# Two stacked cross-attention layers: queries, keys and maxima split into high and low halves, scores and maxima from single-pass products

## The chip, the cores and the metric

The kernel runs on one core of a Trainium2 chip. The time is the device time of one execution in microseconds (us). Three runs of the kernel before gave 947.76 to 949.83 us, with a median of 949.11 us.

## The reference

```python
def layer(x, ctx, Wq, Wk, Wv, Wo, bo):          # x 32x256x320, ctx 32x77x512
    q = heads(x @ Wq)                            # 20 heads of 16 channels
    k, v = heads(ctx @ Wk), heads(ctx @ Wv)
    p = softmax(q @ k.T / sqrt(16), axis=-1)     # 256 x 77 for each head
    return merge_heads(p @ v) @ Wo + bo + x
x = layer(x, ctx, *L0)
x = layer(x, ctx, *L1)
```

All inputs and outputs are float32. The extra key and value weights of the two modules (object, others, ip) meet no rows here, since the context has 77 positions, and they add nothing.

## The kernel before, in words

**Units.** One unit is one layer for one pair of the 32 batch entries: 16 pairs by two layers are 32 units, numbered `u` in an order in which layer 1 of a pair follows its layer 0 by several units. A unit's 20 heads lie in five groups `g` of four head pairs. A head pair takes 32 partitions, so that one group fills the 128 partitions: row group `j` (32 partitions) holds the two heads `e` = 0 and 1 of one pair, 16 channels each.

**Steps of a unit.** `keys` and `keys_rest` project the context to keys (tile kR, by way of the PSUM banks psk). `queries`, or `outputs_and_queries` together with the output projection of the unit three places earlier, project x to queries (tile q0; banks psq and psy). `mask_keys` (L257) makes kT, keys with the other head's 16 rows zeroed, for the maxima. `less_keys` (L267) makes kM, which has the same zeros but a row of minus ones in one of the other head's rows. `maxima` (L455) multiplies 128 queries at a time (as weights) by kT into the banks psm, and VectorE reduces them to the largest score of each query. `turn` (L484) transposes those maxima and sends them by eight DMAs into one row of q0 and q1, each of which holds all the query channels; that row meets the minus ones of kM. So `scores` (L497) yields score minus maximum (banks pss) from one float32 product for each head, ScalarE takes exp into pT, `products` multiplies by the values (banks po), and `divide` and `turn_back` normalise and transpose into oT. q1 is a DMA copy of q0 (lines 339, 349, 385).

**Products.** Each float32 product appears in the profile as two pairs of a weight load (LDWEIGHTS, on the engine row PEld) and a matmul. Four products that use different row groups (or different 32-column strips) run beside each other; below, four such records make a *round*. A group's scores are eight products, or four rounds of 256 columns with 77-column weights. The maxima of one half of a group (`h`, ten to a unit, 128 queries each) are four products, or two rounds of 154 columns with 128-column weights. A unit has ten such halves.

**Order.** `tc.manual_schedule()` leaves the order to the program. It is written out in *slots*: `at(slot, where, step)` files a step, and within a slot steps run in this order:

```python
order = (
    "load", "maxima", "turn back", "turn", "scores", "values", "rest", "back", "full", "last",
)
```

`start(u)` is the slot of a unit's first scores; four units take 17 slots. Queries of unit u are made at the end ("full") of slot s = start(u-2), and its maxima follow from slot s+1 on, two or three halves to a slot, once the unit before has had its own. All engines run their instructions in this order, each waiting on semaphores. TensorE, ScalarE (ACT), VectorE (DVE) and GpSimd (POOL) have a queue each. SyncE (SP) issues nearly all DMAs, in order too, so that a DMA that waits for its data holds those behind it. PSUM has eight banks, taken in turn: four for psm, four for pss, one for po, and so on. Before unit 0's first scores in slot 0 there are ten slots, from -10 on, that fill the pipeline (the *prologue* below); each makes what a later one needs.

Of the kernel before, what the change touches and what calls it, by code (L numbers as in the profile page):

```python
# [52 lines left out]
F32 = mybir.dt.float32  # L53
AF = mybir.ActivationFunctionType
# [12 lines left out]
SCALE = 1.0 / HD**0.5  # L67

# [26 lines left out]
def xattn_kernel(ctx: ExitStack, tc: tile.TileContext, xT, cT, cP, weights, outT):  # L95
# [16 lines left out]
    def load_x(p):  # L112
        x_sb = io.tile([P, NX], F32, tag="x", name=f"x_{p}", bufs=AHEAD + 3)
        xs[p] = x_sb
        if p == 0:
            for a, b in ((0, NT), (NT, 2 * NT), (2 * NT, NX)):
                nc.sync.dma_start(out=x_sb[:, a:b], in_=xT[p, :, a:b])
        else:
            (nc.scalar if p == 1 else nc.sync).dma_start(out=x_sb, in_=xT[p])

    def load_context(u):
        p = units[u][0]
        c_sb = cs[u] = io.tile([P, NKA, NB * L], F32, tag="c", name=f"c_{u}", bufs=3)
# [33 lines left out]
    stages, maxes = [[], []], []  # L157
    for layer in range(2):
        for i in range(2):
# [3 lines left out]
            stages[layer].append(v)  # L163
    for i in range(2):
        m = const.tile([P, 2 * NG, 32], F32, name=f"max_{i}")
        nc.gpsimd.memset(m, 0.0)
        maxes.append(m)
# [6 lines left out]
    masks = const.tile([P, 2], F32, name="masks")  # L174
    nc.vector.tensor_reduce(masks, r32.rearrange("p (e d) -> p e d", d=HD), AX.X, ALU.add)

    less = const.tile([P, 2], F32, name="less")
    for e in range(2):
        i = HD * (1 - e)
        nc.vector.tensor_scalar_mul(less[:, e : e + 1], r32[:, i : i + 1], -1.0)  # L180
# [76 lines left out]
    def mask_keys(u, t):  # L257

        kR, groups = st[u]["kr"], slice(2 * t, min(2 * t + 2, NG))
        n = groups.stop - groups.start  # L260
        kT = work.tile([P, 2, n, L], F32, tag=f"kT{t}", name=f"kT_{u}_{t}", bufs=2)
        st[u]["k", t] = kT
        engine = nc.gpsimd if u else nc.vector
        for e in range(2):
            engine.tensor_scalar_mul(kT[:, e], kR[:, groups], masks[:, e : e + 1])  # L265

    def less_keys(u):  # L267

        kR = st[u].pop("kr")
        kM = st[u]["km"] = work.tile([P, 2, NG, L], F32, tag="kM", name=f"kM_{u}", bufs=3)  # L270
        for e in range(2):
            nc.gpsimd.tensor_scalar(
                kM[:, e], kR, masks[:, e : e + 1], less[:, e : e + 1], ALU.mult, ALU.add
            )

    def keys(u, t):
        p, layer = units[u]
        w, c_sb = w_sb[layer], cs[u]
        if t == 0:
            st[u]["kr"] = work.tile([P, NG, L], F32, tag="kR", name=f"kR_{u}", bufs=2)  # L280
        kR = st[u]["kr"]
# [9 lines left out]
        nc.scalar.copy(kR[:, 2 * t : 2 * t + 2].rearrange("p g k -> p (g k)"), ps[:, 0 : 2 * L])  # L291
        mask_keys(u, t)

    def keys_rest(u):
# [14 lines left out]
        nc.scalar.copy(st[u]["kr"][:, 4], ps[:, 0:L])  # L309
        mask_keys(u, 2)  # L310

    def new_queries(u):
        st[u]["q"] = [
            work.tile([P, NX], F32, tag=f"q{e}", name=f"q{e}_{u}", bufs=3) for e in range(2)
        ]
        return st[u]["q"][0]

    def queries(u):
# [19 lines left out]
        if u > 0:  # L338
            nc.sync.dma_start(out=st[u]["q"][1], in_=q0)

    def queries_rest(u):
# [3 lines left out]
        q0, q1 = st[u]["q"]  # L345
# [3 lines left out]
        nc.sync.dma_start(out=q1, in_=q0)  # L349

    def outputs_and_queries(u, uq):
# [33 lines left out]
        nc.sync.dma_start(out=st[uq]["q"][1], in_=q0)  # L385
# [44 lines left out]
    def place_vals(u, i):  # L430

        p, layer = units[u]
        if "v" not in st[u]:
            st[u]["v"] = work.tile(
                [P, NB, HEADS // 2, 2, 2, HD], F32, tag="v", name=f"v_{u}", bufs=3
# [19 lines left out]
    def maxima(*parts):  # L455
# [3 lines left out]
        for i, (u, h) in enumerate(steps):  # L459
            g, c = h // 2, h % 2  # L460
            q, kT = of_group(st[u]["q"][0], g), st[u]["k", g // 2]
            for j in range(4):
                r = slice(32 * j, 32 * j + 32)
                nc.tensor.matmul(  # L464
                    ps[j][:, i * 2 * L : (i + 1) * 2 * L],
                    q[r, c * P : (c + 1) * P],
# [365 lines left out]
```

## Time and profile before

| what | value |
|---|---|
| three runs, us | 947.76, 949.11, 949.83 |
| profiled execution: span from first to last instruction, us | 947.2 |
| time of that execution outside its span | not shown by the page; the median of the runs is 1.9 us over the span |
| TensorE matmuls (PE) busy | 940.9 us, 99% |
| TensorE weight loads (PEld) busy | 630.3 us, 67% |
| VectorE (DVE) busy | 533.2 us, 56% |
| ScalarE (ACT) busy | 431.8 us, 46% |
| GpSimd (POOL) busy | 254.0 us, 27% |
| mean granted TensorE clock | 1.000 |
| DMA traffic | 83.78 MB, mean 88 GB/s |
| DMAs issued by SP in the program | 508 |

The profile comes from one execution. Busy time of an engine is the union of its records, so that records beside each other count once. The chain of waits follows the last instruction back to what released it, step by step. The timeline gives each engine's records in order of time, with equal neighbours put together.

### The profile page before, as it was taken

The numbers are of one execution on the slowest core, as the hardware profiler recorded it, in microseconds if no ns is written. First come the engines' busy times: TensorE is split into PE (matmuls) and PEld (weight loads), VectorE is DVE, ScalarE is ACT, GpSimd is POOL, SyncE is SP. The second block draws the span as 40 slices with busy tenths as digits, with TensorE's granted clock in tenths as the row PEclk, the third lists the DMA queues.
The fourth block names the chain that finished last, engine by engine and source line by source line (L and its number), as shares of the span: only waits on it lengthen the run. The fifth ranks groups of instructions, "written<-read, shape, count | busy, mean of one in ns | idle before, by whom it ended". The sixth has DMA issues, their size and how long they took to land.

```text
span 947.2 us, 46546 instructions
## 1 busy us (share of the span) xinstructions
PE 940.9 (99%) x20942; PEld 630.3 (67%) x20942; DVE 533.2 (56%) x1195; ACT 431.8 (46%) x975; POOL 254.0 (27%) x422
## 2 busy tenths in 40 slices
PE   9999999999999999999999999999999999999998
PEld 7666766666666676667766666666667666666654
DVE  3465545655555555555656565655555655665564
ACT  2355343553435544355434455335454454544562
POOL 2233212332123321223322233212332223332211
PEclk9999999999999999999999999999999999999999
DMA  6553112232132321323222222322222221222102
GB/s 228 191 160 111 60 58 61 87 127 62 72 105 68 112 71 69 108 72 99 74 74 94 71 96 74 116 67 90 72 85 90 89 89 37 75 93 63 51 33 85
DMA packets 54825, 83.78 MB, mean 88 GB/s; under 512 B 15780, under 2 KB 36580, under 8 KB 54626
## 3 DMA queue, kind: packets, MB, share of 16 engines
q1 hardware_dynamic: 53674, 78.29, 25.4%
q8 instruction: 165, 2.70, 1.2%
q10 hardware_dynamic: 952, 2.50, 0.7%
q14 instruction: 34, 0.28, 0.1%
HBM read 35.39 MB, written 10.49 MB: 48 GB/s over the span
## 4 chain that ended last, share of the span: by engine, by line
PE 99%; DVE 0%; issue 0%
PE po L524 17%; PE psy L194 15%; PE pss L504 15%; PE psq L194 15%; PE psm L464 11%; PE psv L194 9%; PE psk L194 7%; PE psy L228 4%; PE psq L228 4%; PE psk L302 2%; PE warm L185 0%; PE psv L418 0%; DVE max L474 0%; DVE x L566 0%; DVE ones L152 0%
## 5 line engine op out<-in xcount | busy, mean ns | idle before, releaser
L510 ACT ACTIVATE pT<-pss 77x512 f32<-77x512 f32 x640 | 324.4, 593 | 191.3 <-PE pss L504 190.4
L474 DVE TENSOR_REDUCE max<-psm 128x6 f32<-128x462 f32 (+2 forms) x512 | 248.5, 550 | 242.7 <-PE psm L464 242.7
L545 POOL TENSOR_TENSOR normal<-turned,inv 128x256 f32<-128x256 f32 x160 | 99.1, 620 | 655.6 <-DVE inv L540 655.6
L524 PE MATMUL po<-pT,v 77*32 77x256 f32 x2560 | 165.9, 384 | 0.1
L194 PE MATMUL psy<-oT,w 128*32 128x256 f32 (+1 forms) x3072 | 164.4, 380 | 0.0
L504 PE MATMUL pss<-q,kM 32*77 32x256 f32 x2560 | 163.9, 376 | 0.0
L194 PE MATMUL psq<-x,w 128*32 128x256 f32 (+1 forms) x3072 | 151.5, 379 | 0.0
L194 PEld LDWEIGHTS psy<-oT,w 128*32 128x32 f32 (+1 forms) x3072 | 88.2, 108 | 63.6 <-issue 14.8
L536 DVE STREAM_TRANSPOSE turned<-po 128x512 f32<-128x512 f32 x160 | 109.2, 682 | 34.8 <-PE po L524 34.8
L524 PEld LDWEIGHTS po<-pT,v 77*32 77x32 f32 x2560 | 72.3, 109 | 80.2 <-DVE max L474 34.0
L194 PEld LDWEIGHTS psq<-x,w 128*32 128x32 f32 (+1 forms) x3072 | 86.1, 109 | 53.1 <-ACT pT L510 0.9
L265 POOL TENSOR_SCALAR kT<-kR,masks 128x154 f32<-128x154 f32 x186 | 111.7, 612 | 20.2 <-ACT kR L291 20.2
L504 PEld LDWEIGHTS pss<-q,kM 32*77 32x77 f32 x2560 | 98.8, 141 | 26.8 <-DVE oT L559 4.0
L464 PE MATMUL psm<-kT,q 32*128 32x154 f32 x2560 | 115.4, 306 | 0.0
L464 PEld LDWEIGHTS psm<-kT,q 32*128 32x128 f32 x2560 | 89.7, 183 | 32.7 <-issue 24.8
L566 DVE SCALAR_TENSOR_TENSOR x<-psy,w,x 128x256 f32<-128x256 f32 x160 | 69.2, 478 | 73.2 <-PE psy L194 72.0
L194 PE MATMUL psv<-w,cv 128*32 128x160 f32 x2432 | 93.6, 299 | 0.3 <-DVE max L474 0.3
L559 DVE STREAM_TRANSPOSE oT<-normal 128x256 f32<-128x256 f32 x160 | 67.4, 433 | 43.1 <-POOL normal L545 43.1
L381 ACT COPY q<-psq 128x256 f32<-128x256 f32 x28 | 10.4, 372 | 162.0 <-PE psq L228 162.0
L194 PEld LDWEIGHTS psv<-w,cv 128*32 128x32 f32 x2432 | 77.9, 110 | 4.3 <-DVE max L474 0.7
L194 PE MATMUL psk<-c,w 128*32 128x154 f32 x2048 | 78.8, 294 | 0.0
L194 PEld LDWEIGHTS psk<-c,w 128*32 128x32 f32 x2048 | 66.2, 110 | 11.9 <-DVE max L474 0.6
(35 smaller groups left out, 449.0 us busy)
## 6 DMA issues: line engine op xcount, KB each, us to landing
q<-q SPq DMA_DIRECT2D x32, 640.0 KB
c<-in_cP_dram SPq DMA_DIRECT2D x32, 308.0 KB
cv<-in_cT_dram SPq DMA_DIRECT2D x38, 256.0 KB
out_dram<-x SPq DMA_DIRECT2D x15, 640.0 KB
x<-in_xT_dram SPq DMA_DIRECT2D x14, 640.0 KB
v<-stage SPq DMA_DIRECT2D x26, 192.5 KB
q<-mT SPq DMA_DIRECT2D x254, 5.0 KB
w<-in_w_dram ACTq DMA_DIRECT2D x2, 640.0 KB
```

The source lines that it names most:

```text
L194: nc.tensor.matmul(out[m : m + 32], lhsT[:, m : m + 32], rhs, **flags)
L228: nc.tensor.matmul(ps[o : o + 32, 0:S], lhsT, rhs, **flags)
L265: engine.tensor_scalar_mul(kT[:, e], kR[:, groups], masks[:, e : e + 1])
L464: nc.tensor.matmul(ps[j][:, i * 2 * L : (i + 1) * 2 * L], q[r, c * P : (c + 1) * P], kT[r, :, g % 2, :], start=True, stop=True,)
L474: nc.vector.tensor_reduce(maxes[u % 2][:, first : first + n, 2 * j : 2 * j + 2], ps[j][:, at * 2 * L : (at + n) * 2 * L].rearrange("p (c e ...
L504: nc.tensor.matmul(ps[j][:L, e * S : (e + 1) * S], kM[r, e, g, :], q[r, :], start=True, stop=True,)
L510: nc.scalar.activation(st[u]["p", g][j][:L], ps[j][:L], AF.Exp, scale=SCALE)
L524: nc.tensor.matmul(po[o : o + 32, e * S : (e + 1) * S], vpad[:L, b, pair, e].rearrange("p a d -> p (a d)"), pT[j][:L, e * S : (e + 1) * S] ...
L536: nc.vector.transpose(turned[:, 0 : 2 * S], po)
L545: nc.gpsimd.tensor_tensor(normal.rearrange("p q e d -> p e q d"), outs, inv.unsqueeze(3).broadcast_to([P, 2, S // 32, HD]), ALU.mult,)
L559: nc.vector.transpose(of_group(st[u]["o"], g), normal)
L566: nc.vector.scalar_tensor_tensor(x, ps[:, 0:S], w_sb[layer]["b"][:, 0, t : t + 1], x, ALU.add, ALU.add)
```

## The change

Each query and key value is split on the chip into a high half, rounded to the dtype float32r (`F32R`), and the low half, the value minus the high one, also float32r. A head's 32 rows then hold 16 channels twice: the queries as high, low, high, low, and the keys once as high (both rows) and once as low (both rows). A product of two float32r operands is one pass, and two such products, one with each half of the keys, make all four partial products of one head. The zeroed rows and the masks go away. The maxima are split likewise into high and low; they lie in rows of their own (`max_rows`), and one further product of 512 columns with weights of minus ones (`less`) subtracts them in the same bank. The host permutes the columns of the query and key weights so that a pair's two heads alternate.

- `keys` and `keys_rest` copy into the low half of one constant tile `k_halves`. `split_keys` splits it (GpSimd; VectorE for unit 0) and `spread_keys` sends it by four DMAs into the tile kS.
- Queries go into `halves` (one buffer). `split_queries` splits it in two parts (columns 0 to 511, and 512 to 1279), `spread_queries` sends each part by four DMAs into the tile q.
- `maxima` becomes 16 products of 78 columns for each half `h` in place of four of 154. `scores` becomes 16 products of 256 columns and four of 512 in place of eight of 256.
- `turn` splits the maxima on VectorE (two copies, two subtractions), transposes 256 columns in place of 320, and issues four DMAs in place of eight.
- Maxima of a unit may start in slot start(u-2)+2, one later than before; keys are made earlier or at other places, and several buffers are fewer: x from 7 to 6, c, v and oT from 3 to 2, mT from 2 to 1.

```diff
+LP = L + 1
-    x_sb = io.tile([P, NX], F32, tag="x", name=f"x_{p}", bufs=AHEAD + 3)
+    x_sb = io.tile([P, NX], F32, tag="x", name=f"x_{p}", bufs=AHEAD + 2)
...
+maxes = const.tile([P, 2, 4, 32], F32, name="maxes")
+max_rows = []
 for i in range(2):
+    m = const.tile([P, 2, 512], F32R, name=f"max_rows_{i}")
...
+k_halves = const.tile([P, NG, 2, LP], F32R, name="k_halves")
...
+less = const.tile([P, 4, L], F32R, name="less")
...
+def split(engine, high, low):
+    engine.tensor_copy(high, low.bitcast(F32))
+    engine.tensor_tensor(low, low.bitcast(F32), high.bitcast(F32), ALU.subtract)
+
+def split_keys(u):
+    k = k_halves
+    split(nc.gpsimd if u else nc.vector, k[:, :, 0, 0:L], k[:, :, 1, 0:L])
+
+def spread_keys(u):
+    kS = st[u]["k"] = work.tile([P, 2, NG, 2, LP], F32R, tag="kS", name=f"kS_{u}", bufs=3)
+    for e in range(2):
+        for r in range(2):
+            nc.sync.dma_start(
+                out=kS.bitcast(F32).rearrange("(d r) e g h k -> r e d (g h k)", r=2)[r, e],
+                in_=k_halves.bitcast(F32).rearrange("(d e) g h k -> e d (g h k)", e=2)[e],
+            )
+
+def split_queries(u, a, b):
+    x = st[u]["halves"]
+    split(nc.gpsimd if u else nc.vector, x[:, 0, a:b], x[:, 1, a:b])
+
+def spread_queries(u, a, b):
+    for e in range(2):
+        for h in range(2):
+            nc.sync.dma_start(
+                out=st[u]["q"].bitcast(F32).rearrange("(d h) e n -> h e d n", h=2)[h, e, :, a:b],
+                in_=st[u]["halves"].bitcast(F32).rearrange("(d e) h n -> e h d n", e=2)[e, h, :, a:b],
+            )
...
 # maxima
-        for j in range(4):
-            nc.tensor.matmul(ps[j][:, i * 2 * L : (i + 1) * 2 * L],
-                q[r, c * P : (c + 1) * P], kT[r, :, g % 2, :], start=True, stop=True)
+        g, c = h % NG, h // NG
+        for e in range(2):
+            q, kS = of_group(st[u]["q"][:, e], g), st[u]["k"]
+            at = (2 * i + e) * LP
+            for half in range(2):
+                for j in range(4):
+                    r = slice(32 * j, 32 * j + 32)
+                    nc.tensor.matmul(ps[j][:, at : at + LP], q[r, c * P : (c + 1) * P],
+                        kS[r, e, g, half, :], start=(half == 0), stop=(half == 1))
...
 # turn
+    for t in range(2):
+        ...
+        nc.vector.tensor_copy(high.bitcast(F32R), new)
+        nc.vector.tensor_tensor(low, new, high, ALU.subtract)
+    nc.vector.transpose(mT, maxes.rearrange("p t y i -> p (t y i)"))
+    for a in range(4):
+        nc.sync.dma_start(out=max_rows[u % 2]..., in_=mT[32 * a : 32 * a + 32]...)
...
 # scores
 for e in range(2):
-    for j in range(4):
-        nc.tensor.matmul(ps[j][:L, e * S : (e + 1) * S], kM[r, e, g, :], q[r, :],
-            start=True, stop=True)
+    q = of_group(st[u]["q"][:, e], g)
+    for half in range(2):
+        for j in range(4):
+            nc.tensor.matmul(ps[j][:L, e * S : (e + 1) * S], st[u]["k"][r, e, g, half, 0:L],
+                q[r, :], start=(e + half == 0), stop=False)
+for j in range(4):
+    nc.tensor.matmul(ps[j][:L], less[r, g % 4, :], max_rows[u % 2][r, g // 4],
+        start=False, stop=True)
...
 # slots
-    s = start(u - 2)
+    s = start(u - 2) - 2 * (u in (2, NU - 1))
...
-        k = (0, 1, 2) if u == 2 else (s - 2, s - 1, s + 1)
+        k = (s, s + 1, s + 1) if u == 2 else (s - 2, s - 1, s - 1)
...
+        at(k[2] + 1, "split", lambda u=u: split_keys(u))
+        at(k[2] + 2, "load", lambda u=u: spread_keys(u))
...
+        at(s + 1, "load", lambda u=u: spread_queries(u, 0, NT))
+        at(s + 1, "load", lambda u=u: spread_queries(u, NT, NX))
...
+def ready(u):
+    return {2: 1, NU - 1: end - 9}.get(u, start(u - 2) + 2)
...
-        and start(left[0][0] - 2) < slot
+        and ready(left[0][0]) <= slot
...
 at(-10, "last", lambda: queries(0))
+at(-9, "load", lambda: spread_queries(0, 0, 2 * NT))
 for u, slot in ((0, -9), (1, -4)):
     ...
+    at(slot, "last", lambda u=u: split_keys(u))
+    at(slot + 1, "load", lambda u=u: spread_keys(u))
...
+at(-6, "load", lambda: spread_queries(0, 2 * NT, NX))
...
 at(-4, "last", lambda: queries(1))
+at(-3, "load", lambda: spread_queries(1, 0, NX))
...
-    "load", "maxima", "turn back", "turn", "scores", "values", "rest", "back", "full", "last",
+    "load", "maxima", "turn back", "turn", "scores", "values", "rest", "back", "split", "full", "last",
```

## The prediction

> **What bounds the kernel now.** I read the page's busy times and chain first, then the groups by shape, then the timeline in slivers of 30 to 50 ns, and last the timeline of one unit and of the prologue.
>
> ```profile
> PE 940.9 (99%) x20942; PEld 630.3 (67%) x20942; DVE 533.2 (56%) x1195; ACT 431.8 (46%) x975; POOL 254.0 (27%) x422
> ...
> PE 99%; DVE 0%; issue 0%
> PE po L524 17%; PE psy L194 15%; PE pss L504 15%; PE psq L194 15%; PE psm L464 11%; PE psv L194 9%; PE psk L194 7%; PE psy L228 4%; PE psq L228 4%; PE psk L302 2%; PE warm L185 0%; PE psv L418 0%; DVE max L474 0%; DVE x L566 0%; DVE ones L152 0%
> ```
>
> TensorE's matmuls are the chain from end to end: whatever shortens or lengthens a round, or stops TensorE, goes into the time in full. Scores (pss) are 15%, maxima (psm) 11%. The groups by shape (busy, mean ns of one):
>
> ```profile
> L504 PE MATMUL pss<-q,kM 32*77 32x256 f32 x2560 | 163.9, 376 | 0.0
> L464 PE MATMUL psm<-kT,q 32*128 32x154 f32 x2560 | 115.4, 306 | 0.0
> L464 PEld LDWEIGHTS psm<-kT,q 32*128 32x128 f32 x2560 | 89.7, 183 | 32.7 <-issue 24.8 <-DVE inv L540 3.8 <-DVE oT L559 3.4
> L265 POOL TENSOR_SCALAR kT<-kR,masks 128x154 f32<-128x154 f32 x124 | 82.5, 676 | 20.2 <-ACT kR L291 20.2
> L272 POOL TENSOR_SCALAR kM<-kR,masks,less 128x385 f32<-128x385 f32 x64 | 41.8, 661 | 8.5 <-ACT kR L309 8.5
> L545 POOL TENSOR_TENSOR normal<-turned,inv 128x256 f32<-128x256 f32 x160 | 99.1, 620 | 655.6 <-DVE inv L540 655.6
> ```
>
> Two records stand for each float32 product, and matmuls overlap, so the price is the distance between rounds. Record by record, rounds start 215 ns apart in pss (256 columns, each streamed twice), 131.5 in psm (154 columns twice, 128-column weights), 130 in psk (154 columns twice, 32-column weights) and 65 in psk's last tile (77 columns twice). Psm and psk agree, so psm is paced by streaming, not by its weights, but only just. The start of a psm stage shows what a weight load costs by itself (three answers of the timeline; start, length):
>
> ```profile
> 400.46 0.20 PEld L464 LDWEIGHTS psm<-kT,q 32*128 32x128 f32 x4 [0.25 <-DVE inv L540]
> ...
> 400.57 0.34 PEld L464 LDWEIGHTS psm<-kT,q 32*128 32x128 f32 x8
> ...
> 400.70 0.33 PEld L464 LDWEIGHTS psm<-kT,q 32*128 32x128 f32 x8
> ```
>
> No round of the stage streams before its first load is in, and the second load into each row group starts only at 400.57, 108 ns later by the records. (Products' 32-column loads follow each other after 28 ns.) From 400.70 on loads are 131 ns apart, held by the matmuls, since each load starts when the matmul before it in its row group does. So a round with 128-column weights can't be shorter than about 109 ns, however little it streams.
>
> **Part 1, scores: -34.1 us.** Before: 160 groups x 4 rounds x 215 ns = 137.6. After: per group four rounds of 256 columns streamed once, 108 ns (half of 215), and one of 512 columns, 215: 647 ns, x 160 = 103.5. Weights of 77 columns, by the slope from 28 ns at 32 to 108 at 128, load in 65 ns, under 108. That the split operands stream once is the change's claim; no row shows it. Bounds: 108 and 215 a round. I take 108, because the program as built holds one load and one matmul for each split product (24,142 pairs in all: 8,320 split products once, 7,911 others twice).
>
> **Part 2, maxima: +55.3 us.** Before: 320 halves x 2 rounds x 131.5 = 84.2. After, each half has two heads times two key halves: 4 rounds, each streaming only 78 columns once (half of the 65 ns row: 33) but loading 128 columns of queries afresh, though the second load of a pair is the same. At 109 ns: 320 x 4 x 109 = 139.5. Bounds: 35 ns, if loads of split operands were hidden (44.8, so -39.4), and 131.5, the row of today's psm (168.3, so +84.1). I take 109: the load's own row, same partitions and columns. Halving the streaming doubles the loads, and loads become the limit.
>
> The Trainium skill, "TensorE: Matmul & The Clock Gate", section "Back-to-back issue gap", gives about 81 ns for each pair of load and matmul at 128 columns; by that estimate maxima would be 103.7 and the forecast 36 us lower. The 108 ns in this trace speak against it.
>
> TensorE's own work thus grows by 21.2 us.
>
> **Part 3, the way from queries to maxima.** Before, psm reads the tile that ScalarE copied; the q-to-q DMA lies beside. Now copy, split on GpSimd, four or eight DMAs and landing come between. Prices: cast 1.72 ns an element (661/385), subtraction 2.42 (620/256); an SP issue 0.54; a 640 KB q-to-q copy lands 3.0 us after its issue starts, 1.2 of it before the first packet. One unit:
>
> ```profile
> 131.98 0.80 ACT L384 COPY q<-psq 128x256 f32<-128x256 f32 x2 [0.94 <-PE psq L194]
> 133.71 0.80 ACT L384 COPY q<-psq 128x256 f32<-128x256 f32 x2 [0.92 <-PE psq L194]
> 133.99 1.07 PE L464 MATMUL psm<-kT,q 32*128 32x154 f32 x24
> 134.53 0.54 SPq L385 DMA_DIRECT2D q<-q  x1
> ...
> 138.09 4.78 SPq L491 DMA_DIRECT2D q<-mT  x8
> ...
> 140.50 1.07 PE L464 MATMUL psm<-kT,q 32*128 32x154 f32 x24
> ```
>
> The first 512 columns are copied at 132.78 and split at 134.9 (0.88 + 1.24); the other 768 at 138.1 (1.32 + 1.86); the last of four DMAs is issued at 139.7 and lands at 141.4 (1.2, and 0.5 for 192 KB). The unit's first maxima are now due in the slot after next, here at 140.50, some 140.2 with shorter scores. TensorE waits 1.3 us. Other slots are longer; I charge 1.3 in half of 28 units: +18. Bounds: 0 (GpSimd twice as fast) and 45.
>
> In the prologue nothing covers it:
>
> ```profile
> 14.25 1.87 PE L464 MATMUL psm<-kT,q 32*128 32x154 f32 x48
> ...
> 30.34 0.80 ACT L337 COPY q<-psq 128x256 f32<-128x256 f32 x2 [0.92 <-PE psq L194]
> ...
> 30.62 1.60 PE L464 MATMUL psm<-kT,q 32*128 32x154 f32 x40
> ...
> 43.81 1.07 PE L464 MATMUL psm<-kT,q 32*128 32x154 f32 x24
> ```
>
> Today each of these starts at once. Unit 0: keys copied at 12.5, VectorE's splits done at 13.7, nine issues end near 17.6, landing near 19.5 to 20.5: +6. Unit 1: copies end at 31.1, split at 34.7, last issue 36.3, landing 38.4: +7. Unit 2: the same with eight query DMAs, then a key split, an x load and four key DMAs, some 11.5 us in all, of which 3.9 lie under a key projection, maxima of unit 1 and one score group: +8. A fourth wait is in the order: `turn(2)` is filed in slot 4, ahead of `scores(0, 4)`, and both use max_rows[0], so that group's last product waits for unit 2's reductions, transpose and four DMAs: about +6. Unit 3 and small waits: +5. Together +32; bounds 20 (splits at half price) and 45.
>
> The Trainium skill, same page, section on the HAM clock gate, says that a TensorE idle for about 3.4 us falls back to half clock until it has again been busy as long; the trace shows half speed only in the first 5 us. By that estimate these four waits cost some 7 us more.
>
> **Part 4, small.** VectorE's reductions (four in 2.3 us) free the banks that `products` takes; scores between them end 0.2 us sooner, so about 45 stages wait 0.2: +9, of 0 to 20. The last unit has fewer slots from queries to maxima: +4, of 0 to 8.
>
> **At nothing.** GpSimd loses 153.5 us (L265, L272) and gains 6.9 a unit, 214: 314 in all, 30%. VectorE gains about 0.7 a unit, staying under 60%. SP issues 730 DMAs for 508, 394 us at 0.54; behind its wait for the splits stand context, x and value transfers, needed slots later. DMA traffic rises by about 1.5 MB a unit, to 130 MB or 127 GB/s, against 228 in the busiest slice now. Fewer buffers: two units' v and oT are live at a time. If these covers went, value DMAs behind SP would be late first, at some 2 us a unit.
>
> **Sum.** -34.1 + 55.3 + 32 + 18 + 9 + 4 = +84.2. The profiled execution spans 947.2, 1.9 under the runs' median of 949.1, so 1031.4 becomes 1033. About 0.2% (2 us) can be told from no change.
>
> **Rivals.**
> - *Faster: loads of split operands are hidden.* For: the second load of each pair repeats the first; against: the 108 ns row. Rounds of 35 ns make TensorE's work 73.5 shorter; with the 63 of waits, 939. It decides below a round of 43 ns. Chance 0.07.
> - *The waits are covered* and only TensorE's +21.2 counts: 970. For: slots of 4 to 6 us; against: in-order queues in the prologue. 0.09.
> - *Short split products keep the pace of float32*, 131.5 a round: +28.8, 1062. For: psm's row itself. 0.15.
> - *The change doesn't do what it says: two passes each.* Scores then take 160 x (4 x 215 + 430) = 206.4, 103 more: 1136. 0.06.
> - My forecast: 0.60; what I can't name 0.03.
>
> The range from 968 to 1085 takes in the waits' lower end, 131.5 ns rounds with more waiting, and leaves out the fast and the two-pass rival. Faster 0.08, same 0.02, slower 0.90.
>
> **What would show it.** Right: 128-column loads about 109 ns apart through each psm stage, pss rounds near 108, psm's busy time near 170 us; TensorE idle for 6 to 8 us three or four times before 110 us, and for about a microsecond ahead of some psm stages later. Wrong: psm rounds far under 100 or pss rounds at 215; or psm waiting for no DMA.

## The result, and the profile after

The changed kernel takes **1101.66 us** (median of 1097.10, 1100.99, 1102.34 and 1103.18), against 949.11 before: a ratio of **1.160, 95% interval 1.157 to 1.162**. Its profiled execution spans 1095.3 us, 148.1 more than the 947.2 of before. The direction was forecast (chance of slower 0.90), the size was not: 1033 was said, and the range ended at 1085.

First the page: busy times, the granted clock in 40 slices of the span, and the chain of waits by engine and line.

```profile
PE 1029.3 (94%) x24142; PEld 720.3 (66%) x24142; DVE 560.8 (51%) x1323; ACT 433.1 (40%) x975; POOL 285.7 (26%) x361
...
PEclk8876999999999999999999989998999999998899
...
PE 79%; DMA 6%; POOL 6%; SPq 4%; DVE 3%; issue 1%; ACT 1%; POOLq 0%
```

TensorE held 99% of the chain before; now queries' DMAs, GpSimd's split and SP's issues stand in it. The clock row had a 9 in every slice; now it begins with 8876 and has eights later. This is the row before:

```profile
PEclk9999999999999999999999999999999999999999
```

TensorE is "busy" 88 us more, but part of that is the same work at a lower clock. Groups by shape (busy, mean ns of one, idle before and its releasers):

```profile
L486 PE MATMUL psm<-kS,q 32*128 32x78 f32 x5120 | 183.3, 291 | 46.9 <-DMA q<-halves 31.8 <-DMA kS<-k_halves 13.3 <-issue 1.4
L536 PE MATMUL pss<-q,kS 32*77 32x256 f32 x2560 | 115.2, 292 | 1.8 <-issue 1.0 <-DVE turned L573 0.3 <-DVE x L603 0.3
L542 PE MATMUL pss<-max_rows,less 32*77 32x512 f32 x640 | 68.2, 405 | 9.8 <-DMA max_rows<-mT 9.8
L266 POOL TENSOR_TENSOR halves<-halves 128x768 fp32r<-128x768 f32 x31 | 56.7, 1829 | 2.5
L265 POOL CAST halves<-halves 128x768 fp32r<-128x768 f32 x31 | 25.6, 824 | 0.0
```

GpSimd's split was priced from other rows: the subtraction of 768 columns as it came (1.86 us said, 1.83 measured), the cast too high (1.32 said, 0.82). The loads of a maxima stage, in two slivers of the timeline:

```profile
478.61 0.31 PEld L486 LDWEIGHTS psm<-kS,q 32*128 32x128 f32 x8
...
478.72 0.31 PEld L486 LDWEIGHTS psm<-kS,q 32*128 32x128 f32 x8
```

Loads, and with them rounds, follow each other after 112 ns (109 was said), though a product streams only 78 columns. One steady unit and the prologue, from the timeline (start, length; the bracket holds the idle time before and what ended it):

```profile
478.51 1.09 PE L486 MATMUL psm<-kS,q 32*128 32x78 f32 x32
481.16 0.42 PE L486 MATMUL psm<-kS,q 32*128 32x78 f32 x8 [1.57 <-DMA q<-halves]
482.37 0.42 PE L486 MATMUL psm<-kS,q 32*128 32x78 f32 x8 [0.79 <-DMA q<-halves]
```

```profile
19.44 0.65 PE L486 MATMUL psm<-kS,q 32*128 32x78 f32 x8 [4.32 <-DMA kS<-k_halves]
49.70 0.65 PE L486 MATMUL psm<-kS,q 32*128 32x78 f32 x8 [6.01 <-DMA q<-halves]
78.20 0.65 PE L486 MATMUL psm<-kS,q 32*128 32x78 f32 x8 [8.78 <-DMA kS<-k_halves]
107.82 0.72 PE L542 MATMUL pss<-max_rows,less 32*77 32x512 f32 x4 [6.89 <-DMA max_rows<-mT]
```

These are the four prologue waits of the forecast. They also show its hole: after the first three, eight products take 0.65 us where 0.42 is normal, and after the last the four products that subtract the maxima take 0.72 us where 0.40 and 0.43 are normal (at 476.03 and 483.09 us). The windows view gives the clock of such stretches (start:end, length, busy time of each engine, clock, DMA share, GB/s):

```profile
16.50:30.20 13.70, 8.88 (x144) 7.79 (x148) 4.56 (x8) 0.29 (x1) 0.00 (x0) 0.50 0.49 168
47.20:57.50 10.30, 6.92 (x116) 6.26 (x120) 3.82 (x8) 0.00 (x0) 0.00 (x0) 0.50 0.33 122
71.10:98.40 27.30, 19.94 (x276) 14.37 (x280) 11.78 (x28) 6.49 (x13) 1.24 (x2) 0.50 0.59 191
113.00:1095.30 982.30, 947.09 (x22548) 659.03 (x22544) 524.06 (x1237) 411.57 (x922) 264.93 (x330) 0.97 0.36 118
```

In all TensorE ran at half clock for **116 us** in 17 stretches, 58 of them before 113 us; before the change there was none after the start. Each lasts a multiple of 3.41 us, but for the last, which the end of the kernel cuts short, and TensorE is busy for 96 us of them.

**Where 148.1 us went**, from start-to-start distances of products at full clock and without waits, and from the gaps between records. The scores hold the way from their last product to the value products at its length of before (so 155.7 where the prediction has 137.6); what it grew by is the step's row:

| | before | after | us |
|---|---|---|---|
| maxima | 95.9 | 144.1 | +48.2 |
| scores | 155.7 | 126.9 | -28.8 |
| other work | 688.2 | 687.8 | -0.4 |
| step from a group's last score product to its first value product (mean), 160 times | 313 ns | 390 ns | +12 |
| gaps between TensorE's records | 6.3 | 66.0 | +59.7 |
| half clock: 96 us of busy time at half rate | 0 | 48 | +48 |
| not placed (perhaps the first part of the waits, which lies under the record of the product before; not shown) | | | +9 |

### The profile page after: what moved, and what is told of

Its sections match the earlier page's. It is cut to its first block, busy times and chain, and to the rows that moved or that the text cites. A ratio compares the mean times of both kernels' runs of the same rounds, so it can differ in the third digit from the quotient of the medians.

```text
span 1095.3 us, 53635 instructions
## 1 busy us (share of the span) xinstructions
PE 1029.3 (94%) x24142; PEld 720.3 (66%) x24142; DVE 560.8 (51%) x1323; ACT 433.1 (40%) x975; POOL 285.7 (26%) x361
## 4 chain that ended last, share of the span: by engine, by line
PE 79%; DMA 6%; POOL 6%; SPq 4%; DVE 3%; issue 1%; ACT 1%; POOLq 0%
PE po L561 13%; PE psy L200 13%; PE psm L486 11%; PE psq L200 11%; PE pss L536 7%; PE psv L200 6%; PE psk L200 6%; DMA q<-halves 5%; POOL halves L266 4%; PE psy L234 4%; PE pss L542 3%; PE psq L234 3%; SPq L292 3%; POOL halves L265 2%; DVE m L498 1%
## 5 line engine op out<-in xcount | busy, mean ns | idle before, releaser
L498 DVE TENSOR_REDUCE m<-psm 128x6 f32<-128x462 f32 (+2 forms) x512 | 248.8, 553 | 328.3 <-PE psm L486 328.3
L486 PE MATMUL psm<-kS,q 32*128 32x78 f32 x5120 | 183.3, 291 | 46.9 <-DMA q<-halves 31.8
L486 PEld LDWEIGHTS psm<-kS,q 32*128 32x128 f32 x5120 | 166.8, 197 | 83.5 <-issue 53.8
L561 PE MATMUL po<-pT,v 77*32 77x256 f32 x2560 | 179.2, 407 | 2.5
L536 PE MATMUL pss<-q,kS 32*77 32x256 f32 x2560 | 115.2, 292 | 1.8 <-issue 1.0
L200 PE MATMUL psv<-w,cv 128*32 128x160 f32 x2432 | 102.1, 317 | 0.0
L266 POOL TENSOR_TENSOR halves<-halves 128x512 fp32r<-128x512 f32 (+1 forms) x62 | 96.1, 1550 | 5.0
L265 POOL CAST halves<-halves 128x512 fp32r<-128x512 f32 (+1 forms) x62 | 44.4, 717 | 202.1 <-ACT halves L402 174.4
L200 PE MATMUL psk<-c,w 128*32 128x154 f32 x2048 | 87.3, 314 | 0.0
L536 PEld LDWEIGHTS pss<-q,kS 32*77 32x77 f32 x2560 | 80.0, 146 | 9.1 <-issue 1.2
L200 PEld LDWEIGHTS psk<-c,w 128*32 128x32 f32 x2048 | 72.1, 118 | 15.3 <-issue 3.1
```

What stands on the lines that cost most here:

```text
L200: nc.tensor.matmul(out[m : m + 32], lhsT[:, m : m + 32], rhs, **flags)
L266: engine.tensor_tensor(low, low.bitcast(F32), high.bitcast(F32), ALU.subtract)
L486: nc.tensor.matmul(ps[j][:, at : at + LP], q[r, c * P : (c + 1) * P], kS[r, e, g, half, :], start=(half == 0), stop=(half == 1),)
L498: nc.vector.tensor_reduce(st[u]["m"].rearrange("p e h j -> p h e j")[:, first : first + n, :, j], ps[j][:, at * 2 * LP : (at + n) * 2 * LP ...
L536: nc.tensor.matmul(ps[j][:L, e * S : (e + 1) * S], st[u]["k"][r, e, g, half, 0:L], q[r, :], start=(e + half == 0), stop=False,)
L561: nc.tensor.matmul(po[o : o + 32, e * S : (e + 1) * S], vpad[:L, b, pair, e].rearrange("p a d -> p (a d)"), pT[j][:L, e * S : (e + 1) * S] ...
```

## The experiments

Those with an interval were timed in three or more rounds, the others once. The four runs of the changed kernel lie 6 us apart, and their granted clocks of 0.941 to 0.947 stand for 130 to 116 us of half clock, so a single run that differs from it by no more than that shows nothing. The theory (A): the clock follows the share of time in which the array streams; waits and load-paced maxima together push it down. Rivals: only an idle stretch near 3.4 us does it (B), or the single-pass form as such (C).

**1. No waits.** Maxima and the subtraction read constant tiles.

```diff
-    q[r, c * P : (c + 1) * P], kS[r, e, g, half, :],
+    still_q[r, :], still_k[r, :],
...
-    less[r, g % 4, :], max_rows[u % 2][r, g // 4], ...
+    less[r, g % 4, :], still_m[r, :], ...
```

> The maxima's products read constant tiles instead of the spread queries and keys, and the product that subtracts the maxima reads a constant tile of zeros, so TensorE waits for none of these transfers; the maxima are then not those of the data. TensorE's instructions, their sizes and their order are those of the changed kernel. Theory A (the waits and the load-paced maxima together leave the array streaming too small a share of the time, and the clock falls): without waits only the maxima's stages are sparse, a slot holds enough other work, clock about 1.00, idle under 15 us, time 975 to 990 us. Theory B (only an idle stretch of TensorE near 3.4 us makes the clock fall): the same, 975 to 990. Theory C (single-pass products, or short products by themselves, lower the clock, whatever the waits): the half clock stays for some 100 us and the time is about 1040 us. If the clock isn't what cost the 69 us, the time is 1101.7 - 60 = 1042 us.

Measured: 1008.15 us (ratio to before 1.061, 1.059 to 1.063), 18 over the forecast's end. Gaps fell from 66.0 to 12.4 us. In the profiled runs, 53.6 us fewer gaps and half of the 59 us less busy time at half clock make 83 of the 85 us between the two spans. Half clock remained for 37.5 us, with 0.05 us of gaps in it, so that A's expectation of a clock near 1.00 without waits failed too. The windows view of this run, with the window before a later fall of the clock, at 945.34 us, in the last line:

```profile
47.60:51.00 3.40, 2.66 (x63) 1.96 (x58) 2.28 (x4) 2.04 (x4) 1.74 (x3) 1.00 0.56 220
51.00:78.40 27.40, 27.35 (x401) 19.08 (x397) 17.08 (x42) 8.75 (x18) 2.48 (x4) 0.50 0.58 177
78.40:113.00 34.60, 34.54 (x817) 23.35 (x812) 14.50 (x31) 17.55 (x39) 10.76 (x14) 1.00 0.36 122
...
941.93:945.34 3.41, 3.22 (x77) 2.62 (x81) 2.57 (x8) 2.45 (x6) 0.62 (x1) 1.00 0.66 254
```

TensorE is busy for 27.35 of 27.40 us and yet at half clock: this is where maxima and scores of units 0 to 2 follow each other with little else. It begins behind a window in which three single products of the maxima stand 0.55 us apart, waiting up to 0.25 us each for VectorE to empty a bank. The later fall comes behind a window in which TensorE was busy for 3.22 of 3.41 us and no gap was longer than 0.19 us. B falls as the only cause: load-paced stages alone can bring the half clock. The Trainium skill, "TensorE: Matmul & The Clock Gate", section "HAM oscillation — how this bites in real kernels", gives the rule of no idle gap above about 3.4 us; this stretch has no gap above 0.25 us near it and breaks that rule. The same page's next section, "A second HAM failure mode: psum-queue depth-cycling", tells of micro-idles that make the clock swing, which is nearer to what is seen here.

**2. The same, streaming more.** Experiment 1, its maxima products 256 columns wide instead of 78, same loads and order.

```diff
-    ps[j][:, at : at + LP], still_q[r, :], still_k[r, :],   # 78 columns
+    ps[j][:, 256 * e : 256 * e + 256], still_q[r, :], still_k[r, :],   # 256
```

> The kernel without transfers ahead of TensorE (constant tiles in the maxima's products and the subtraction, so the maxima are not those of the data), whose maxima products now stream 256 columns instead of 78. That kernel without the widening took 1008 us and still showed the half clock for 37.5 us, 27.3 of them in one stretch from 51 to 78 us with 0.05 us of idle in all of it. Theory A (clock follows the share of time that the array streams): no sparse stage is left, the half clock is gone (under 5 us), and the time is 1009.9 - 18.8 (half of 37.5) + 20 (1,280 rounds, 16 ns longer) = about 1011 us, clock 1.00. Theory C (single-pass products lower the clock by themselves): the half clock stays at 30 us or more, time 1030 or more. Theory B (idle near 3.4 us) has already no place for the 27 us; it would need an idle stretch that the records hide.

Measured: 1014.45 us. The clock row of the page:

```profile
PEclk9999999999999999999999999999999999999999
```

Half clock fell to 6.8 us, 3.4 of them in the prologue, where there were 27.3. The 1,280 rounds stream three times as much and stay near their loads' pace (120 ns a round where it was 112), so they cost little. Single-pass products alone bring hardly any half clock: C falls. With the waits gone and the maxima streaming, the clock stays up, as A says.

**3. The wide products with the waits.**

```diff
-    ps[j][:, at : at + LP], ..., kS[r, e, g, half, :],
+    ps[j][:, 256 * e : 256 * e + 256], ...,
+    kS.rearrange("p e g h k -> p (e g h k)")[r, first : first + 256],
```

> Each of the maxima's products streams 256 columns of the same spread keys instead of 78; loads, waits and order are those of the changed kernel, and the maxima are then over other columns. If the rounds are paced by their weight loads (112 ns now), they grow only to the 119 ns of the scores' 256-column rounds: 5,120 products in 1,280 rounds, +9 us of work; if they are paced by streaming they triple. Theory A (clock follows the share of time that the array streams): the half-clock time falls from 117 us to under 50, the stretch from 78 to 98 us goes first, and the time falls to about 1040 to 1075 us although more work is done. Theory B (only idle stretches near 3.4 us): the waits are the same, half-clock time stays near 117 us or grows, since a 256-column product takes 213 ns at half clock; time 1110 to 1150 us.

Measured: 1095.85 us. TensorE's work grew by 13.5 us (958.8 to 972.2 at full clock), yet the time did not rise: this one run lies 6 us under the median of the changed kernel and 1 us under its shortest run. Half clock fell from 116 to 83 us, not below 50; what is left follows the waits. As forecast, the long stretch from 71 to 98 us broke up, here with a clock of 0.98:

```profile
79.00:93.00 14.00, 13.29 (x308) 9.71 (x304) 12.20 (x30) 6.43 (x13) 1.87 (x3) 0.98 0.38 111
```

The time was forecast too low, because half clock stayed at 83 us and the work grew by more than the 9 us allowed; the gaps (62 us) are nearly those of before.

**4. Waits alone, in float32.** The kernel before, its maxima reading the queries' tile that a DMA fills.

```diff
-    q, kT = of_group(st[u]["q"][0], g), st[u]["k", g // 2]
+    q, kT = of_group(st[u]["q"][1], g), st[u]["k", g // 2]
```

> The kernel before, with one edit: the maxima read the queries' second tile, which a DMA fills, instead of the first, which ScalarE fills. Work on every engine is that of before, all float32; the result is the same. The DMA lands about 3 us after its issue begins, so TensorE waits some 1 to 3 us once per unit (32 units), 40 to 90 us in all. Theory A (share of streaming in a window): a window with 2 us of wait streams 0.4 or less, so the half clock follows the waits here as well, 3.4 us or more each time: 40 to 100 us of half clock, time 1010 to 1080 us, the loss well above the idle time. Theory B (idle near 3.4 us only): hardly any half clock while waits are under 3 us, time 990 to 1040 us, the loss equal to the idle time. Theory C (single-pass products): no half clock, time as in B.

Measured: 1147.95 us, 198 more than before for one changed index. Waits and clock:

```profile
PE psm L464 <- DMA q<-q: 121.0, 32, 4.4
...
PEclk8888999889988999898899989999989999999899
```

The waits were mis-sized (3.1 to 4.4 us each, not 1 to 3), so the time lies above the forecast. Two readings hold: a kernel of float32 products alone gets half clock (171 us of it, after 30 of the 32 waits), against C; and the loss, 198 us of span, is well above the 120 us of added gaps. It doesn't tell A from B, since every wait came out near 3.4 us, where B too has the half clock.

**5. Shorter steady waits, two ways.** First a shorter split, on VectorE:

```diff
-    split(nc.gpsimd if u else nc.vector, x[:, 0, a:b], x[:, 1, a:b])
+    split(nc.vector, x[:, 0, a:b], x[:, 1, a:b])
```

> The queries of every unit are split on VectorE (0.43 and 0.69 us for 512 columns in its own rows) instead of GpSimd (0.61 and 1.27; 0.83 and 1.83 for 768), so the queries land about 1.8 us sooner in each unit, while VectorE has 2.8 us more per unit. If the steady waits for the queries are real, the waits of L486 after 113 us (about 36 us of idle later on) fall by half or more. Theory A: short half-clock stretches after waits go with them, 15 to 30 us more; time 1055 to 1080 us. Theory B: the later stretches follow waits of 1 to 3 us only by chance, so only the idle time goes: 1080 to 1090 us. If VectorE's extra work delays the banks instead: no change or slower, 1100 to 1110 us.

Measured: 1090.93 us. Waits of L486 after 113 us fell from 24.8 to 15.3 us, but value products now wait 14.8 us there (2.5 before), mostly for VectorE's reductions to empty a bank: the total stays at 32. The run doesn't tell A from B. Then the maxima of every fourth unit one slot later, with no change of work:

```diff
-    return {2: 1, NU - 1: end - 9}.get(u, start(u - 2) + 2)
+    return {2: 1, NU - 1: end - 9}.get(u, start(u - 2) + (3 if u > 3 and u % 4 == 1 else 2))
```

> The changed kernel with the maxima of every fourth unit (u % 4 == 1) filed one slot later; no work changes. Of the steady waits for spread queries (24.8 us of idle at L486 after 113 us, 1 to 2.7 us at a time in two of every four units) the half that belongs to these units goes, about 12 us. Theory A (short waits and load-paced rounds together bring the half clock): the half-clock stretches behind them go too, 15 to 30 us of half clock, 8 to 15 us of time: 1075 to 1082 us. Theory B (only idle near 3.4 us): the stretches have another cause and stay: about 1090 us. If the slots that now take the maxima wait as long: 1100.

Measured: 1060.26 us, 41 less and below both forecasts. Waits of L486 after 113 us fell from 24.8 to 2.5 us: the neighbouring unit's went as well. The waits after 113 us, first of the changed kernel, then of this one (those of L486 for queries are 23.3 of the 24.8 and 2.3 of the 2.5 us):

```profile
PE psm L486 <- DMA q<-halves: 23.3, 27, 2.7
PE pss L542 <- DMA max_rows<-mT: 2.9, 3, 1.4
...
PE pss L542 <- DMA max_rows<-mT: 8.0, 9, 1.5
PE psm L486 <- DMA q<-halves: 2.3, 4, 0.9
```

The window of the steady part:

```profile
113.00:900.00 787.00, 773.63 (x19137) 547.47 (x19132) 432.61 (x1046) 343.97 (x775) 225.84 (x280) 1.00 0.39 127
```

Half clock after 113 us fell from 58 to 11 us. The waits taken away were 0.2 to 2.7 us long, none near 3.4: short waits did bring the half clock, and they cost more than their own length. Since waits for the maxima's rows grew, the gaps as a whole fell by only 14 us, and the spans of the two profiled runs differ by 37; half of the 45 us less half clock is the rest.

**6. Three tiles for the maxima's rows.**

```diff
-    for i in range(2):   # max_rows
+    for i in range(3):
...
-    max_rows[u % 2]
+    max_rows[u % 3]
```

> The changed kernel with three tiles for the maxima's rows in place of two, so that scores(0, 4) no longer shares a tile with turn(2), filed ahead of it. The 6.9 us wait of L542 at 101 us goes. Theory A: the half clock that follows it (105 to 112 us) goes too, another 3 us: time 1101.7 - 10 = about 1091 us. Theory B (no idle stretch over 3.4 us, no half clock) says the same here. If the wait only moves to the next product that needs these rows: 1098 to 1102.

Measured: 1100.27 us, a miss. The 6.89 us wait went, and prologue gaps fell from 29.7 to 21.8 us, but half clock after 113 us rose from 58 to 82. In all this run had 133 us of half clock, next to 116 to 130 in the runs of the changed kernel, so that most of the rise is no more than their own spread. Perhaps steady waits of 1 to 2 us lie at the edge where the clock falls or not, and a shift of the work moves some across; one run doesn't show it.

**7. Half of the maxima's products.** Only the keys' high half.

```diff
-    for half in range(2):
+    for half in range(1):
```

> The maxima take the keys' high half alone: one product per head and half instead of two, 2,560 instead of 5,120 products; a row's maximum is then that of slightly different scores, and the shift in the exponent is still the same for all keys of a row. TensorE's work falls by 640 rounds of 112 ns, 71.7 us. Waits for queries and keys stay and begin sooner, by at most the work left out in the slots ahead (0.9 us a slot), so idle grows by up to 30 us. Theory A: the sparse stages halve, half-clock time falls to 70 to 110 us; time 1030 to 1055 us. Theory B: half-clock time stays or grows with the waits; time 1040 to 1065 us. If maxima rounds were hidden behind something else, the time stays near 1100 us.

Measured: 1061.59 us, 40 less, for 70.8 us less work (958.8 to 888.0). Gaps rose from 66 to 84 us and half clock from 116 to 147. A's figure of 70 to 110 us failed, and what B expected came out, in half clock and in time: this run by itself speaks for B, which experiments 1 and 5 rule out as the only cause. I had counted the sparse stages that go but not that less work between waits can leave each window emptier; that this is the reason was not tested.

**8. Split scores with unsplit maxima.** Two kernels in which no maxima product waits for a DMA: ScalarE's copy (or a rounded one) and masked keys feed the maxima, queries are spread later for the scores alone.

```diff
-    q, kS = of_group(st[u]["q"][:, e], g), st[u]["k"]   # spread halves, 16 products
+    q, kT = of_group(st[u]["raw"], g), st[u]["k", g // 2]   # float32, 4 products
...
-    at(s + 1, "load", lambda u=u: spread_queries(u, 0, NT))
+    at(late_by, "split", lambda u=u: split_queries(u, 0, NX))
+    at(late_by + 1, "load", lambda u=u: spread_queries(u, 0, NX))
```

> Scores split as in the change; maxima as before (float32, queries as ScalarE copied them, keys masked on GpSimd), so no maxima product waits for a DMA; queries are split and spread three slots later, for the scores alone. By the steps of the forecast: scores 155.7 - 126.9 = 28.8 us less, maxima unchanged, the step from scores to products 0.075 us longer in 160 places (+12), some 5 us of waits in the prologue. Theory A and B: clock 0.99 or more; time 949 - 29 + 12 + 5 = about 937 us (925 to 945). If the split scores cannot pay whatever the maxima do (waits move to the scores' first product): 960 or more.

> As the kernel with split scores and unsplit maxima, but the maxima take one single-pass product per half: ScalarE writes the queries' high half itself (rounded), VectorE makes the low half from PSUM, and the masked keys are rounded too. A row's maximum is then that of scores rounded differently, and still the same for all keys of a row. Rounds stream 156 columns once (65 ns) behind a 112 ns load, instead of 131.5: 640 rounds x 19.5 = 12.5 us less work than its float32 twin. Theory A: the maxima's stages stream 0.58 of the time, so in the prologue between 47 and 80 us, where little else runs, half clock may come for up to 25 us (12 us lost), elsewhere none: time 925 to 940, equal to the twin or a little less. Theory B: no half clock without a wait near 3.4 us: the twin's time less 12 us. VectorE's 1.5 to 2 us more per unit may hold back banks: up to +15 us.

Measured: 1076.28 (ratio 1.133, 1.131 to 1.136) and 1057.45 us (1.113, 1.108 to 1.118). Both forecasts failed by over 100 us, for two reasons that I had built in. Of the first kernel, the waits and the timeline:

```profile
PE pss L556 <- DMA max_rows<-mT: 51.7, 7, 8.8
PE pss L550 <- DMA q<-halves: 25.6, 12, 6.1
```

```profile
185.43 2.65 SPq L535 DMA_DIRECT2D max_rows<-mT  x4
...
189.73 0.71 PE L556 MATMUL pss<-max_rows,less 32*77 32x512 f32 x4 [7.10 <-DMA max_rows<-mT]
```

Maxima filed one slot earlier put turn of unit u+2 ahead of the scores of unit u that share its max_rows tile: the fault of `turn(2)` once every four units. And queries sent in one piece land late: issued from 512.19 to 516.25 us, waited for until 524.35. Half clock came with it (124 and 140 us). The expectation of the second kernel, and that of its mended form below, also have a wrong term: a float32 half takes two rounds of 131.5 ns, a single-pass one takes one of 112, so the saving is 320 x 151 = 48 us, not 12.5. With order and issue mended:

```diff
-    return {...}.get(u, start(u - 2) + 1)
+    return {...}.get(u, start(u - 2) + 2)
-    late_by = start(u - 2) + 5
+    late_by = start(u - 2) + 4      # with float32 maxima; 3 with single-pass maxima
...
+    # single-pass maxima only: queries' high half cast on GpSimd behind ScalarE's copy
+    split_queries(uq, (0, NT), (NT, NX))
```

> The kernel with split scores and float32 maxima (1076 us) with two filings changed and no work: maxima one slot later (turn then stands behind the scores that used its tile, so the 51.7 us of waits of the subtraction's product go), and the queries' split and DMAs one slot sooner (39 us of waits of the first score product shrink to 15 or less). Theory A: of its 123.5 us of half clock most follow these two waits and go: 1076 - 52 - 25 - 40 = about 960 (945 to 980). Theory B: the 7 us waits bring half clock and go with it, the 3 us ones don't: 965 to 990. If split scores need the waits whatever the order: 1050 or more.

> Split scores; the maxima take one single-pass product per half (queries' high half, cast on GpSimd right behind ScalarE's copy, and masked keys, rounded), filed one slot later than in the two kernels with unsplit maxima run so far, which puts turn behind the scores that its tile blocked (51.7 and 49.6 us of waits of the subtraction's product there); the queries' DMAs for the scores are issued two slots sooner (47.4 us of waits of the first score product there came from their 7 to 8 us on the way). Work: 940 - 28.8 - 12.5 = 898.5; scores to products +12; waits of the first products for banks and queries 20 to 35; ends 6. Theory A: maxima stages stream 0.58 of the time and the scores' waits thin them further, half clock 10 to 40 us, 5 to 20 us of time: 945 to 965 us; without any half clock 935 to 945. If the waits stay as in its predecessor: 1040 or more.

Measured: 974.48 us with float32 maxima (half clock 25 us; within both forecasts), 966.67 with single-pass maxima (ratio 1.017, 1.011 to 1.023; half clock 65 us; 2 us above A's forecast, with more half clock than it said). Filing alone was worth 102 us. Still neither beats the kernel before. In the first, rounds are some 25 us shorter by their distances, but gaps are 20.3 longer, the step from scores to values takes 397 ns instead of 313 (+13), and half clock costs some 12. In the second the largest wait is:

```profile
PE pss L556 <- DVE turned L593: 26.9, 29, 2.1
```

Shorter scores no longer cover VectorE, which empties the banks. Moving turn behind those transposes in VectorE's queue:

```diff
-    at(slot, "rest" if u == 2 else "turn", lambda u=u: turn(u))
+    at(slot, "rest" if u == 2 else "back", lambda u=u: turn(u))
```

> The kernel with split scores and single-pass maxima (966.7 us), with one filing changed: turn (1.3 to 2.6 us of VectorE per unit) stands behind the values' transposes of its slot instead of ahead of them. There the scores' first product waited 26.9 us in 29 places for the transpose that empties a bank of PSUM. Theory A: if turn is what makes that transpose late, some 15 to 25 us of waits go, and with them most of the 44 us of half clock after 113 us (another 15 us): 930 to 950 us. If VectorE is simply short of time in these slots (four reductions of 2.3 us, two transposes), the wait moves to another product: 960 to 970.

Measured: 975.93 us, no faster, and above both forecasts. The wait moved to the value products (28.2 us for the reductions, 25 times). That fits a VectorE that is short of time in these slots; only this one other order was tried.

**9. Only the maxima single-pass, nothing spread.** The kernel before, with queries cast on GpSimd and masked keys rounded:

```diff
+    (nc.gpsimd if u else nc.vector).tensor_copy(st[u]["qh"][:, a:b], st[u]["q"][0][:, a:b])
...
-    q, kT = of_group(st[u]["q"][0], g), st[u]["k", g // 2]   # float32
+    q, kT = of_group(st[u]["qh"], g), st[u]["k", g // 2]   # both float32r
```

> The kernel before with only the maxima changed: queries and masked keys rounded to float32r (GpSimd casts the queries behind ScalarE's copy, the keys' masking writes the rounded form), one single-pass product per half instead of a float32 one; nothing is spread by DMA, scores and all transfers stay as before; x has 6 buffers and oT 2. A row's maximum is then that of rounded scores, the same shift for all keys of a row, as in the kernels with single-pass maxima run so far, whose expectations put the saving at 12.5 us: a float32 half takes two rounds of 131.5 ns, so it is 320 x (263 - 112) = 48 us. Theory A: no wait for a transfer, but maxima's stages stream 0.58 of the time, so half clock only where they stand close together, between 47 and 80 us: up to 15 us of it, 7 us lost; waits for the cast and the banks up to 10: 949 - 48 + 5 to 17 = 906 to 918 us. Theory B: no half clock, 901 to 911. If single-pass products bring the loss by themselves: 940 or more.

Measured: **917.34 us, ratio 0.966 (0.965 to 0.967)**: faster than both kernels, and within A's forecast. Busy times and clock:

```profile
PE 908.3 (99%) x19662; PEld 597.0 (65%) x19662; DVE 534.4 (58%) x1201; ACT 431.9 (47%) x975; POOL 303.2 (33%) x577
...
PEclk9999999999999999999999999999999999999999
```

Gaps are 7.1 us and half clock 3.4. Maxima went from 95.9 to 43.2 us; scores, untouched, rose from 155.7 to 173.0. That the time lies within the forecast is luck in part: the 5 to 17 us that it allowed for half clock and waits were some 2.5, and the 17 us of the scores, which it did not have, took their place. The same dtype gains where it needs no transfer on the path.

## Why the forecast was right in direction and wrong in size

- **Scores, -34.1.** Measured -28.8: rounds of 256 columns take 119 ns where 108 was taken, the first of a group 160. The claim that split operands stream once holds.
- **Maxima, +55.3.** Measured +48.2, at 112 ns a round against 109; they are load-paced, which experiment 2 confirms by streaming three times as much in nearly the same rounds. The difference is smaller than forecast because the maxima before took 95.9 us, not 84.2: the first round of a stage takes longer (238 ns at 400.46 us, against 131.5). The 81 ns of the Trainium skill ("TensorE: Matmul & The Clock Gate", "Back-to-back issue gap") do not hold for these loads, as the row of before had said.
- **Prologue waits, +32.** Measured 29.0 more gaps there, in the four places named: 6, 7, 8 and 6 us said, 4.3 and 1.6, 6.0, 8.8, 6.9 seen.
- **Steady waits and the last unit, +22.** Measured 32, 24.8 of them ahead of the maxima: 0.8 to 2.7 us in about two of every four units, as "1.3 us in half of the units" had it.
- **Banks, +9.** Measured +12, in the step from scores to values, which mostly ends when a reduction on VectorE frees the bank.
- **The step that failed: the clock.** These terms sum to 84 forecast and, with other work and the end of the kernel 1.7 us shorter, to 91 measured. What is missing is 48 to 57 us. The prediction put the clock at nothing in its sum and range; it stood only in the sentences on the skill's page, with "some 7 us more" for four long waits. Measured by busy time at half rate it cost 48 us. Its own numbers held the warning: it worked out rounds of 109 ns that stream 33 ns, and waits of a microsecond in half the units, but asked only whether TensorE stood still for 3.4 us. The runs show half clock also behind waits of 0.8 to 2.7 us, and without the waits for transfers (experiment 1) for 27 us with 0.05 us of gaps in them. Charged so, with half rate in the prologue behind its first wait (95 us) and in one window of 3.4 us behind the waits of 14 units, the sum would have been 1033 + 95/2 + 14 x 3.4/2 = about 1104, and the range would have lain round that. That this comes so near is luck: it charges 71 us for the clock where 48 were measured, and the other terms and what is not placed are 16 us more than forecast.
- **At nothing.** GpSimd was put at 314 us busy and shows 285.7; VectorE at under 60% shows 51%; SP's queue delayed no value DMA that TensorE waited for. That held.

## What to carry to other kernels

Ask of each stage not only how long it takes but how much of it the array streams: a stage of short products behind long loads, or a string of short waits, lowers the granted clock for everything in the next 3.4 us and more, so that a wait can cost twice its length (experiment 5: 14 us of gaps, 37 us of span). Put a new step such as a split or a spread where other work covers it before shortening products, and check which steps a filing order puts ahead of work that shares a tile; here filing alone was worth 102 us. A cheaper form of a product pays first where its operands need no transfer: the maxima, whose exact value doesn't matter as long as all keys of a row share it.

## What the runs showed of the hardware that was not expected

- The clock falls and recovers in steps of 3.41 us. How much of such a window the array streams can be estimated from the records' columns (215 ns for a round of four records with 256 columns in float32, half of that for split or rounded products; the estimate sums to 937 us for the kernel before, which is busy for 941). In the changed kernel it streamed at most 0.41 of each of the 16 windows after which the clock fell, and at least 0.42 of each window after which it stayed full. Over all profiled runs the two overlap: falls come after up to 0.48, and the clock stayed full after as little as 0.35. Busy time parts them worse: the clock fell after windows with TensorE busy for up to 0.94, and stayed full after as little as 0.46.
- In experiment 9 the scores' products are those of before, but in each group the product of one row group starts behind the other three, by 76 ns in the first round and 139 in the last (medians; 7 before), and the group takes 1,097 ns instead of 970; from its last product to the value products it is 304 ns, as before. That takes back 17 us of the maxima's 53. Its cause was not looked for.
